# Four planned durations in the written-out order of a one-core transformer block: the exponential, the SiLU, GpSimd's power and GpSimd's products

## The chip, the cores and the metric

The kernel runs on one core of one Trainium2 chip. The core has a matrix engine (TensorE; PE in the profile, its weight loads PEld), a vector engine (VectorE, DVE), an activation engine (ScalarE, ACT), GpSimd (POOL) and SyncE (SP), which here issues DMAs alone. Each engine works through its own list of instructions in the order in which the program wrote them, and waits on semaphores where it needs another engine's result.

The metric is the device time of one execution in microseconds (us). Three runs before the change took 1913.58, 1913.61 and 1914.87 us; the median is 1913.61.

## The reference

One block with adaptive layer norms: attention over 2 batches of 2048 tokens of width 256, 16 heads with keys of 16 and values of 64, and a gated FFN of hidden width 704 whose inputs and weights are quantised to FP4 in blocks of 16.

```python
mod = (_silu(L0_c) @ L0_wmod).reshape(L0_c.shape[0], 6, 1, -1)
sa, ca, ga, sb, cb, gb = (mod[:, 0], ..., mod[:, 5])
...
h = _layernorm(x, axis=-1) * (1 + ca) + sa
x = x + ga * _L0_attn_ref(h, ...)
h = _layernorm(x, axis=-1) * (1 + cb) + sb
x = x + gb * _L0_ffn_ref(h, ...)

def _L0_attn_ref(x, query_proj, key_proj, value_proj, output_proj):
    q, k, v = ...
    sim = jnp.einsum('bnkh,bmhk->bnhm', q, k)
    attn = jax.nn.softmax(sim * scale, axis=1)      # over the queries
    o = jnp.einsum('bnhm,bmhv->bnhv', attn, v)
    return jnp.einsum('bnhv,dhv->bnd', o, output_proj)

def fp4_linear(x, w):
    return jnp.einsum('bsk,nk->bsn', fp4_quant_dequant(x), fp4_quant_dequant(w))

h = jax.nn.silu(fp4_linear(x, w_gate)) * fp4_linear(x, w_up)
return fp4_linear(h, w_down)
```

The softmax runs over the queries. So for a block of 128 keys of one head, all 2048 queries lie along one row, and the sum of exponentials belongs to the key.

## The kernel before

**The work.** The attention is 512 steps: 2 batches, 16 heads, 16 blocks of 128 keys. In one step (`step` and `scores`):

1. PE multiplies keys by queries, four score matmuls (`ps`) into two double PSUM banks of 1024 scores each, a half step per double bank. There are three such banks (room `s`).
2. DVE scales each half into the SBUF tile `e` (room `e`, five of them) and takes the row's minimum with it, in one pass: 1024 such passes.
3. POOL joins the two minima (`mn`).
4. ACT takes the exponential of the whole row of 2048 in place, with its sum `z` from the accumulator.
5. DVE takes the reciprocal `rz`, POOL scales the 64 values by it (`vn`).
6. PE multiplies `vn` by `e` into the output sums (`o`), eight matmuls in the trace.

All else is woven between these steps: the projections to q, k (`qk`) and v (`v`), copies of finished sums (`osb`), output projections (`op`), the weights' quantisation during the first batch, the second batch's first norms, and, during the second batch's attention, the first batch's FFN (`ffn_stats`, `ffn`: rows `gate`, `up`, `h2t`, `dn`, 16 tiles of 128 tokens). The second batch's FFN comes last, after the last step, with nothing beside it (`project_last`, `tail_norm`, `tail`, `tail_part`: rows `pg`, `pu`, `dn`).

**The order.** Every operation is a step of some generator, a `Chain`, with a due time counted in attention steps. `Order.run` is a planner that runs when the program is built. It keeps a clock for each engine, and for every chain whose next operation could go it works out the earliest start from the engine's clock, the end of the chain's last operation, a latency (0.2 us across engines) and a free room (a buffer). On each engine it looks at all that could start within a small time of the earliest (`patience`: PE 0.12, DVE 0.04, ACT 0.05 us) and takes the one due first. What it picks is emitted at once, so the order of the picks is the order of each engine's instructions. The chip then follows that order whatever its own durations are.

The planner's durations come from `Queue.estimate`, by engine, operation and size. Four more things hang on them:

- `scores` opens a visit to the scores with up to two half steps and lets it grow to three (`GROUP`), if a bank comes free within `PATIENCE` = 0.1 us of the time at which the visit would end.
- `Either` and `Best` give the planner a choice of engine: copies out of PSUM by ACT or DVE, products by POOL or DVE. `Best` takes the first unless it would end more than a margin later than the second. The margins are 0.5 us for copies and for the last FFN, 2 us for the first FFN and 3 us for the weights.
- SiLU and the exponential need different ACT tables. A change of table is planned at 1.3 us.
- An operation of POOL, and one of DVE with two inputs in SBUF (`shares`), reserves a shared `port` from its start to its planned end. Another such operation is not planned to start before that end.

**The operations whose planned duration the change touches.** The exponential is in `step` (an activation with a bias from SBUF and an accumulated sum). Two other activations accumulate: `Square` in `ffn_stats` and a copy in `projected`, both in the last FFN. SiLU stands in `ffn` (all 704 columns), `tail` (704) and `tail_part` (352). The power is in `inverse_root`: `G.tensor_tensor(r, v, half_root..., ALU.pow)` on 128 x 4, 128 x 3 or 128 x 1 numbers, from variance to the layer norm's root, followed at once by four small DVE operations (tiles `ln1`, `ln2`; `a` is the first norm, `f` the FFN's). POOL's products are all other `G.tensor_tensor`: in `quantize`, `quantize_exactly`, `ffn_apply`, `finish`, `load_wo` and `weight_tail`.

Each instruction that the planner emits bears the line of the call in `make`, L275; the tiles' names tell them apart.

## Time and profile before

| what | value |
|---|---|
| median of the runs | 1913.61 us |
| span of the profiled execution, first to last instruction | 1911.2 us |
| granted TensorE clock | 1.000 of full speed |
| exponential, 128 x 2048 | 512 times, mean 2003 ns, and 512 accumulator reads, mean 186 ns |
| SiLU, 704 columns, first FFN | 16 times, mean 757 ns |
| power, 128 x 4 | 15 times, means 1032 (first norms) and 1087 ns (FFN) |
| product on POOL, 128 x 704, plain and with a factor per block | means 1693 and 1390 ns |
| product on POOL, 128 x 256, plain and with a factor per block | means 733 and 623 ns |

An engine's busy time is the time in which an instruction of it was under way. Matmuls overlap in their pipeline, so a busy PE can still lose time between two kinds of matmuls. The rows of groups give the tiles written and read, the count, the busy time, the mean of one, and the idle time of the engine just before, with what ended it. Rows of the timeline give the start, the length, the engine, the line, the operation, the tiles and how many in a row were merged; a bracket at the end is the engine's idle time before it.

### The profile page before, as it was taken

The page shows a single profiled execution, that of the slowest core. Times are in us where ns is not written, and L with a number is a line of the kernel's source. Part 1 is how long each engine was busy: PE and PEld are TensorE (multiplying, and loading weights), DVE is VectorE, ACT ScalarE, POOL GpSimd, SP SyncE. Part 2 cuts the span into 40 slices and gives each one's busy share as a digit, 9 for nine tenths or more (in the row PEclk, how much of TensorE's full clock was granted, in tenths as well). Part 3 has the DMA queues.
Part 4 walks back from the last instruction along what each step waited for, and adds up shares of the span by engine and source line. Part 5 has one row for each costly group of instructions (what it writes and reads, how often), then busy time and mean ns, then how long its engine had stood idle before and what let it go on. Part 6 is the DMA issues. An engine that isn't in the chain of part 4 may idle for free.

```text
span 1911.2 us, 30108 instructions
## 1 busy us (share of the span) xinstructions
PE 1886.2 (99%) x10184; PEld 782.0 (41%) x10184; DVE 1691.7 (89%) x3975; ACT 1326.9 (69%) x1463; POOL 652.2 (34%) x1421
## 2 busy tenths in 40 slices
PE   9999999999999999999999999999999999999998
PEld 5333333343333333334334443434434333335666
DVE  5999999999999998888898788798788988997997
ACT  4687677776777677766777567766676867786433
POOL 1343333333334332113445345454353211231222
PEclk9999999999999999999999999999999999999999
DMA  6422021112120223211111201210111111101011
GB/s 215 104 63 56 30 55 49 45 27 51 34 60 21 51 56 94 78 39 45 31 37 48 61 31 47 51 42 10 39 37 37 42 34 34 34 7 39 9 17 20
DMA packets 42249, 89.83 MB, mean 47 GB/s; under 512 B 6384, under 2 KB 24432, under 8 KB 38128
## 3 DMA queue, kind: packets, MB, share of 16 engines
q1 hardware_dynamic: 38720, 83.97, 16.9%
q0 software_dynamic: 2016, 1.84, 0.8%
q10 hardware_dynamic: 1360, 2.10, 0.3%
q8 instruction: 81, 1.33, 0.3%
q14 instruction: 72, 0.59, 0.1%
HBM read 63.51 MB, written 22.81 MB: 45 GB/s over the span
## 4 chain that ended last, share of the span: by engine, by line
PE 88%; DVE 8%; ACT 2%; issue 1%; POOL 0%; ACTq 0%; POOLq 0%
PE o L275 44%; PE ps L275 15%; DVE e L275 6%; PE v L275 6%; PE op L275 5%; PE dn L275 5%; PE qk L275 3%; PE up L275 2%; PE pg L275 2%; PE gate L275 2%; PE pu L275 2%; PE h2t L275 1%; ACT e L275 1%; PE busy L275 1%; PE hq L275 0%
## 5 line engine op out<-in xcount | busy, mean ns | idle before, releaser
L275 DVE TENSOR_SCALAR_CACHE_REDUCE e<-ps 128x1024 f32<-128x1024 f32 x1024 | 1227.8, 1216 | 101.7 <-PE ps L275 82.4
L275 ACT ACTIVATE e<-e,mn 128x2048 f32<-128x2048 f32 x512 | 1025.2, 2003 | 401.4 <-POOL mn L275 397.7
L275 PE MATMUL o<-e,vn 128*64 128x512 f32 x4096 | 992.8, 603 | 6.7 <-POOL vn L275 2.9
L275 PEld LDWEIGHTS o<-e,vn 128*64 128x64 f32 x4096 | 255.9, 136 | 454.6 <-issue 371.4
L275 POOL TENSOR_SCALAR mn<-mn 128x1 f32<-128x1 f32 x512 | 154.2, 301 | 688.4 <-DVE rz L275 314.9
L275 PE MATMUL ps<-q,k 64*128 64x512 f32 x2048 | 369.0, 444 | 2.0 <-DVE e L275 1.6
L275 PEld LDWEIGHTS ps<-q,k 64*128 64x128 f32 x2048 | 160.2, 184 | 345.2 <-DVE e L275 132.3
L275 POOL TENSOR_SCALAR vn<-v,rz 128x64 f32<-128x64 f32 x512 | 166.5, 325 | 295.2 <-DVE rz L275 207.3
L275 PE MATMUL op<-wo,osb 128*64 128x256 f32 (+1 forms) x960 | 125.6, 382 | 1.2 <-DVE x L275 1.0
L275 PE MATMUL v<-wv,ht 128*64 128x256 f32 x1024 | 124.4, 382 | 0.3 <-DVE e L275 0.3
L275 PEld LDWEIGHTS op<-wo,osb 128*64 128x64 f32 (+1 forms) x960 | 74.1, 140 | 60.4 <-issue 22.2
L275 PEld LDWEIGHTS v<-wv,ht 128*64 128x64 f32 x1024 | 71.1, 137 | 65.5 <-issue 26.3
L275 DVE RECIPROCAL rz<-z 128x1 f32<-128x1 f32 x512 | 80.7, 158 | 18.8 <-ACT e L275 17.8
L275 ACT ACTIVATION_READ_ACCUMULATOR e<-e,mn 128x1 f32 x512 | 95.3, 186 | 0.0
L275 DVE DVE_READ_ACCUMULATOR e<-ps 128x1 f32 x1024 | 85.2, 83 | 0.0
L275 ACT COPY osb<-o 64x512 f32<-64x512 f32 x108 | 62.5, 580 | 14.9 <-PE o L275 13.4
L275 PE MATMUL qk<-ht,wqk_sb 128*64 128x512 f32 (+1 forms) x224 | 61.8, 599 | 1.1 <-ACT ht L275 0.9
L275 POOL TENSOR_TENSOR h<-h,m 128x704 f32<-128x704 f32 x32 | 54.2, 1693 | 12.3 <-DVE m L275 5.4
L275 DVE TENSOR_TENSOR x<-op,x 128x512 f32<-128x512 f32 (+1 forms) x59 | 39.8, 674 | 11.6 <-PE op L275 11.2
L275 PE MATMUL dn<-wdb,e 117*128 117x256 f32 (+1 forms) x192 | 45.1, 383 | 4.1 <-ACT e L275 4.0
L275 ACT ACT_TABLE_LOAD x34 | 43.6, 1283 | 4.3 <-issue 3.7
L275 PE MATMUL dn<-wd_t,h2t 117*64 117x256 f32 (+1 forms) x384 | 46.0, 381 | 0.0
(251 smaller groups left out, 1449.7 us busy)
## 6 DMA issues: line engine op xcount, KB each, us to landing
k<-scr SPq DMA_DIRECT2D x124, 256.0 KB, 4.5
scr<-st SPq DMA_DIRECT2D x32, 512.0 KB, 3.1
q<-scr SPq DMA_DIRECT2D x124, 128.0 KB, 5.5
x<-in_x_dram SPq DMA_DIRECT2D x8, 512.0 KB, 4.2
wv<-in_wv_dram SPq DMA_DIRECT2D x8, 256.0 KB, 3.6
wo<-in_wo_dram SPq DMA_DIRECT2D x8, 256.0 KB, 2.7
xt<-in_x_dram SPq DMA_DIRECT2D x4, 512.0 KB, 8.0
out_dram<-h2t SPq DMA_DIRECT2D x16, 128.0 KB, 1.9
```

The lines of the kernel that those rows point to most:

```text
L275: op = Op(self.name, *self.estimate(method, args, kw, lambda: f(*args, **kw)))
```

## The change

Four durations in `Queue.estimate` are replaced. With an accumulated sum an activation's planned duration grows by 0.11 us in place of 0.17. SiLU gets 0.148 us more. A power on POOL gets 1.0 us, whatever its size, where it had 0.08 us plus 0.0023 us a column, or 0.28 us for one column. The fixed part of all other tensor-tensor operations of POOL with more than one column goes from 0.08 to 0.11 us. Nothing else is changed: no operation, buffer, due time, margin or patience.

```diff
@@ -314,15 +314,18 @@
             func = kw.get("func", args[2] if method == "activation" else None)
             table = {AF.Exp: "exp", AF.Silu: "silu"}.get(func)
             t += 0.093 * sum(isinstance(kw.get(k), bass.AP) for k in ("bias", "scale"))
-            t += 0.17 * isinstance(kw.get("accum_out"), bass.AP)
+            t += 0.11 * isinstance(kw.get("accum_out"), bass.AP)
+            t += 0.148 * (func == AF.Silu)
             return t, emit, 0.0, table
         if self.name == "POOL":
             if method == "tensor_scalar":
                 return 0.16 + 0.083 * len(aps[2:]) + n * 0.001, emit
+            if ALU.pow in args:
+                return 1.0, emit
             if n == 1:
                 return 0.28, emit
             spread = any(len(a.ap) > 2 and a.ap[-1][0] == 0 for a in aps)
-            return 0.08 + n * (0.0019 if spread else 0.0023), emit
+            return 0.11 + n * (0.0019 if spread else 0.0023), emit
         if method == "reciprocal":
             return 0.07 + n * 0.0063, emit
         scalars = method == "tensor_scalar" and len(aps) > 2
```

## The prediction

> **What bounds the kernel now.** I read the page first: span, busy time, chain.

> ```profile
> span 1911.2 us, 30108 instructions
> PE 1886.2 (99%) x10184; PEld 782.0 (41%) x10184; DVE 1691.7 (89%) x3975; ACT 1326.9 (69%) x1463; POOL 652.2 (34%) x1421
> PE 88%; DVE 8%; ACT 2%; issue 1%; POOL 0%; ACTq 0%; POOLq 0%
> ```

> TensorE is never out of work for long. So the order in which its work is written out decides, not one slow engine. Next the busy time by stretch: the attention with all that is woven into it (50 to 1742 us), and two stretches of the last FFN.

> ```profile
> 50.00:1742.00 1692.00, 1682.98 (x9272) 640.45 (x9272) 1516.69 (x3502) 1236.55 (x1289) 610.63 (x1370) 1.00 0.17 45
> ...
> 1785.00:1830.00 45.00, 43.07 (x186) 31.10 (x185) 43.98 (x104) 19.83 (x39) 9.51 (x9) 1.00 0.13 15
> 1830.00:1870.00 40.00, 37.52 (x162) 27.27 (x161) 38.98 (x96) 14.14 (x23) 11.65 (x10) 1.00 0.12 14
> ```

> The columns after the length are PE, PEld, DVE, ACT, POOL. In the attention PE stands still for 9.0 us of 1692. In the last FFN DVE is the full engine: 82.96 of 85 us.

> What then fills the attention, if not waiting? The timeline shows turns between scores (ps) and weighted sums (o).

> ```profile
> 499.96 2.00 ACT L275 ACTIVATE e<-e,mn 128x2048 f32<-128x2048 f32 x1
> ...
> 501.46 0.96 PE L275 MATMUL ps<-q,k 64*128 64x512 f32 x6
> ...
> 501.87 0.19 ACT L275 ACTIVATION_READ_ACCUMULATOR e<-e,mn 128x1 f32 x1
> ...
> 502.35 2.80 PE L275 MATMUL o<-e,vn 128*64 128x512 f32 x12
> ...
> 505.08 1.07 PE L275 MATMUL ps<-q,k 64*128 64x512 f32 x6
> ...
> 508.80 0.73 PE L275 MATMUL ps<-q,k 64*128 64x512 f32 x4
> ...
> 509.46 1.94 PE L275 MATMUL o<-e,vn 128*64 128x512 f32 x8
> ```

> Six ps hold PE for 502.35 - 501.46 = 0.89 us, four for 509.46 - 508.80 = 0.66, so two cost 0.23 and a visit costs 0.66 - 0.46 = 0.20 on top. Twelve o last 2.80 and eight 1.94, so four cost 0.86; twelve (2.58) hold PE for 505.08 - 502.35 = 2.73, 0.15 on top. A turn to the scores and back thus costs 0.35 us. Counted over the whole timeline there are 462 visits to the scores (117 of six matmuls, 328 of four, 17 of two), 12 to 16 for each of the 32 heads: some 160 us.

> **The change part by part.** It gives the planner other costs and adds, removes and moves no instruction by itself: the same 30108 can come out in another order, and where two engines may do an operation the choice can flip. No DMA is added. A moved instruction moves SP's and POOL's queues with it, but no wait on a load stands among PE's waits after 50 us, so I cost that at nothing; if a head's load came late its cover is the stretch of some 16 steps by which it is issued ahead.

> Exponential: planned at 0.05 + 2048/1200 + 0.04 + 0.093 + 0.17 = 2.06 us, then 2.00. In the fence above the accumulator read ends 2.10 after the exponential began, but it overlaps: the next free moment of ACT comes after 501.87 - 499.96 = 1.91 plus about 0.09, so 2.00 is right for ACT's queue. For the reader behind it the last step shows it undisturbed: the exponential began at 1740.01, the reciprocal of its sum at 1742.14, 2.13 later; the plan allowed 2.06 + 0.20 and will allow 2.20. So 0.07 of cover is left of 0.13. What is late if the cover goes is vn on POOL, and then PE:

> ```profile
> PEld o L275 <- POOL vn L275: 27.4, 65, 1.7
> ...
> PE o L275 <- POOL vn L275: 2.9, 5, 1.3
> ```

> 65 times the weight load of an o began on the release by vn, so an o planned 0.06 earlier costs up to 65 x 0.06 = 3.9 us. The other end is a gain: ACT looks 512 x 0.06 = 31 us emptier to the planner, and copies may leave DVE for it; if one in ten of the 54 that DVE does from PSUM for v and osb (0.69 each) left, DVE would have 3.5 us less. I take +2.0, half of the first, since DVE's row is not PE's.

> Power: planned 0.09 us for the four-wide ones (0.28 for the one-wide), then 1.00. Measured 1.03 (17 in all; the three-wide 0.86, the one-wide 0.58). What planning it short does is seen here:

> ```profile
> 998.92 1.04 POOL L275 TENSOR_TENSOR ln1f<-ln0f,half_root 128x4 f32<-128x4 f32 x1 [0.81 <-DVE ln0f L275]
> ...
> 999.92 1.68 POOL L275 TENSOR_TENSOR h<-h,m 128x704 f32<-128x704 f32 x1
> 999.99 1.64 DVE L275 TENSOR_TENSOR ln2f<-ln1f 128x4 f32<-128x4 f32 x1 [1.15 <-POOL ln1f L275]
> ...
> 1002.83 0.50 PE L275 MATMUL ps<-q,k 64*128 64x512 f32 x2 [0.97 <-DVE e L275]
> ...
> 1003.97 0.49 PE L275 MATMUL ps<-q,k 64*128 64x512 f32 x2 [0.64 <-DVE e L275]
> ```

> DVE stood 1.15 us for the power with the next pass over scores queued behind it, then its small product took 1.64 beside a POOL product, and PE lost 0.97 + 0.64 = 1.61. With 1.00 planned, that pass goes ahead: -1.6. By tile, DVE waited for the power 3.0 us (5 times) in the FFN norms and 2.8 (3 times) in the first ones, so -5.8 is the lower end; the upper is the power in the first tile of the last FFN, planned 0.42 too long, which PE covers (its projections run until 1763.45, the tile is ready at 1759.83); uncovered, +0.4. I take -1.6, the only wait that reaches PE beyond doubt.

> The power also reserves the planner's shared port, now for 1.00 instead of 0.09 us, against DVE operations with two SBUF inputs. The row at 1762.77 shows a power of 1.02 us with such an operation of DVE (128x256) starting at 1763.25 and taking its usual 0.42: no block. [...]

> SiLU and products: SiLU 0.64 planned, then 0.79. Before a table load it holds ACT 0.77 (1002.57 to 1003.34), so 16 of them become truer; in the last FFN the next ACT operation came 0.64 after (1806.78 to 1807.42), so 17 become 0.15 too long. [...] Products become 0.03 longer: 1.73 planned against 1.69 measured (704 wide), 0.70 against 0.73 (256). In the last FFN POOL does 13 (seven e, six w) with a margin of 0.5 against DVE: a shift of 0.03 flips some 13 x 0.03/0.5 = 0.8 of them, and an e product on DVE takes 0.89 where DVE is full: +0.7. Ends: 0, and all seven, +6.2. In the attention DVE has 1692 - 1517 = 175 us of cover, so no term.

> New order: the planner takes the earliest start within 0.12 us and the lowest due time, so a shift of 0.06 in 512 steps redraws the attention's order. The trace has no row for a redraw; the nearest are its own heads. Taking each kind's mean spacing inside its stretches as streaming, a head loses 11 to 16 us outside it, with a spread (standard deviation) of 1.2 from head to head; over 30 heads that is 1.2 x root of 30 = 6.6. So -6.6 to +6.6. I take ten visits more, a third of one per head: 10 x 0.35 = +3.5. Two rows make me lean to loss. A third half of scores joins a visit only if DVE frees its bank within 0.1 us; banks come free every 1.22 us, so moving PE 0.06 earlier breaks 5% of the 117 visits of six, about six, which is three visits. And PE's waiting in the attention is only 9.0 us in all, so a redraw has little to win there and no such floor under what it may lose.

> Sum: 2.0 - 1.6 + 0.7 + 3.5 = +4.6. On the execution's own span: 1911.2 + 4.6 = 1915.8; the median of the runs shown, 1913.61, lies 2.4 above the span, so 1918.2.

> **The rivals.** Faster: the power's true length is the whole story. DVE's 5.8 us of standing before the root steps all reach PE, or the prologue's start (2.8 of them lie before 24 us, where PE has no scores yet): 1913.6 - 5.8 = 1907.8. It decides if visits to the scores stay at 462 or fall; each ten fewer give 3.5 more. Against it: of three waits in the first norms PE shows only 1.42 us for xn there.

> No change: the terms cancel and the redraw gives nothing: 2.0 - 1.6 + 0.7 = +1.1, 1914.7. That the changed costs hardly move any choice belongs here. For it: 9 us of waiting leave little to move. Against it: a sum of 30 heads seldom stays near zero.

> Slower by the last FFN alone: its chains plan SiLU 0.15 too long and all seven e products go to the full DVE: 7 x 0.89 = 6.2, 1919.8. Against it: ACT is half idle there, and the 0.5 margin still favours POOL.

> **How the numbers follow.** Forecast (more turns) 0.34; last FFN 0.11; no change 0.22; faster 0.33. Slower has 0.45. 0.2% is 3.8 us, about what a measurement here can tell from no change: 1909.8 to 1917.4 is the same. The slower cases alone span 1917.5 to 1930. The whole range takes the faster end, 1913.6 - 5.8 - 3.5 = 1904.3, so 1904, and at the top the upper ends 3.9 + 6.2 + 6.6 = 16.7, so 1930.

> **What would show it.** Visits of scores: 472 or so against 462; under 455 the forecast is wrong. DVE's wait of 1.15 before the root step near 1000 us gone. PE's loads on vn over 65. The seven e products on POOL: six or seven. PE's 9.0 us of waiting in the attention: a rise over 15 would mean waits, not turns, and a fall below 6 with fewer visits the faster rival.

## The result and the profile after

After the change the kernel takes 1921.88 us (median of four runs, 1921.67 to 1923.63), before 1913.78 (four runs beside it, 1913.58 to 1914.87). The ratio is 1.0042, 95% interval 1.0028 to 1.0056: slower by 8.1 us. The span of the profiled execution went from 1911.2 to 1919.9.

The page of the changed kernel, span and busy time:

```profile
span 1919.9 us, 30085 instructions
PE 1888.7 (98%) x10184; PEld 779.7 (41%) x10184; DVE 1694.3 (88%) x3983; ACT 1325.8 (69%) x1461; POOL 646.8 (34%) x1416
PE 11%; ACT 0%; issue 0%; DVE 0%; ACTq 0%
```

The same work in another order. In the last row the chain of waits was followed over 11% of the span only, so I don't read it, and compare stretches instead. The busy time by stretch of the changed kernel, columns as before (length, PE, PEld, DVE, ACT, POOL, granted clock, DMA):

```profile
50.00:1742.00 1692.00, 1678.71 (x9240) 636.22 (x9234) 1511.33 (x3486) 1229.94 (x1284) 611.36 (x1367) 1.00 0.18 44
1785.00:1830.00 45.00, 42.98 (x183) 30.75 (x182) 43.30 (x101) 17.23 (x27) 6.85 (x7) 1.00 0.11 13
1830.00:1870.00 40.00, 37.28 (x160) 26.52 (x159) 37.99 (x90) 16.59 (x33) 8.63 (x8) 1.00 0.15 17
```

PE now stands still for 13.3 us of these 1692 where it was 9.0. The two stretches don't hold the same work, as the changed order runs later. So, to see where, I cut each trace at PE's own events: the first score matmul, the first of head 13 and of head 16 (heads counted from 0 over both batches, so 16 is the second batch's first), and the last weighted sum.

| stage | before, us | after, us | PE idle before | after | visits before | after |
|---|---|---|---|---|---|---|
| up to the first scores | 38.4 | 40.9 | 4.2 | 3.9 | | |
| heads 0 to 12 | 643.3 | 638.5 | 4.7 | 4.0 | 187 | 191 |
| heads 13 to 15 | 159.0 | 168.4 | 2.0 | 8.4 | 45 | 46 |
| heads 16 to 31 | 904.7 | 904.6 | 2.6 | 2.1 | 230 | 234 |
| last FFN | 165.7 | 167.5 | 7.9 | 9.1 | | |

From the first scores to the last weighted sum PE stands still for 9.4 us before and 14.5 after. The start is 2.5 longer because the changed order puts 16 matmuls of v and two of the modulation ahead of the first scores. Heads 0 to 12, which no longer hold them, are 4.8 shorter. The loss is in heads 13 to 15: +9.4, of which 6.4 is PE standing still. About 1.0 more is four `o` and two transposes that stood in heads 0 to 12 before. Three stretches there, before and then after:

```profile
681.00:737.00 56.00, 53.99 (x278) 18.77 (x274) 49.65 (x122) 43.36 (x50) 17.65 (x42) 1.00 0.25 66
737.00:797.00 60.00, 60.00 (x302) 20.21 (x302) 50.21 (x101) 44.63 (x48) 12.22 (x40) 1.00 0.27 85
797.00:848.00 51.00, 51.00 (x312) 21.45 (x310) 40.95 (x83) 35.42 (x38) 9.04 (x31) 1.00 0.27 67
```

```profile
681.00:737.00 56.00, 51.74 (x270) 18.70 (x268) 50.59 (x122) 40.61 (x44) 15.41 (x39) 1.00 0.24 63
737.00:797.00 60.00, 57.59 (x284) 18.45 (x280) 43.68 (x88) 39.16 (x43) 10.88 (x34) 1.00 0.26 81
797.00:848.00 51.00, 49.27 (x292) 20.16 (x292) 43.41 (x87) 35.08 (x38) 9.12 (x31) 1.00 0.14 37
```

PE loses 2.25, 2.41 and 1.73 us, 6.4 together. In the middle stretch no engine is short of capacity: DVE too does less (43.68 against 50.21 busy). That is the mark of a pipeline that runs too shallow, where each engine waits for the next. The weight loads of the weighted sums say at which link (waits of the weight loads in 737 to 848, total, times, longest), before and then after:

```profile
PEld o L275 <- POOL vn L275: 1.1, 3, 0.4
```

```profile
PEld o L275 <- POOL vn L275: 8.8, 10, 1.9
```

And PE's rows of the timeline, after, in head 14:

```profile
768.72 1.08 PE L275 MATMUL o<-e,vn 128*64 128x512 f32 x4
769.88 0.49 PE L275 MATMUL ps<-q,k 64*128 64x512 f32 x2
...
770.98 1.94 PE L275 MATMUL o<-e,vn 128*64 128x512 f32 x8
773.57 1.08 PE L275 MATMUL o<-e,vn 128*64 128x512 f32 x4 [0.65 <-POOL vn L275]
774.58 0.73 PE L275 MATMUL ps<-q,k 64*128 64x512 f32 x4
775.24 1.94 PE L275 MATMUL qk<-ht,wqk_sb 128*64 128x512 f32 x8
```

PE has done all that was ready and waits for `vn` of the very next step. I put a number on this: the lead, by how many steps the scores already issued are ahead of the weighted sums when a step's first `o` begins, as a mean over a head.

| head | 12 | 13 | 14 | 15 |
|---|---|---|---|---|
| before | 3.78 | 3.47 | 4.41 | 4.91 |
| after | 3.41 | 3.50 | 3.00 | 4.56 |

Both orders lose lead in heads 12 and 13, where the second batch's norms and the last of the weights' quantisation are woven in (DVE is busy for 99% of head 12 in both). The order of before has it back in head 14. In the changed order it falls further in that stretch, to 3.0; there the second batch's `qk` take turns with the scores.

### The profile page after: what moved, and what is told of

Same layout as the page of the kernel before. It is cut to its first block, busy times and chain, and to the rows that moved or that the text cites. A ratio compares the mean times of both kernels' runs of the same rounds, so it can differ in the third digit from the quotient of the medians.

```text
span 1919.9 us, 30085 instructions
## 1 busy us (share of the span) xinstructions
PE 1888.7 (98%) x10184; PEld 779.7 (41%) x10184; DVE 1694.3 (88%) x3983; ACT 1325.8 (69%) x1461; POOL 646.8 (34%) x1416
## 5 line engine op out<-in xcount | busy, mean ns | idle before, releaser
L275 DVE TENSOR_SCALAR_CACHE_REDUCE e<-ps 128x1024 f32<-128x1024 f32 x1024 | 1227.0, 1216 | 102.9 <-PE ps L275 81.5
L275 ACT ACTIVATE e<-e,mn 128x2048 f32<-128x2048 f32 x512 | 1025.3, 2003 | 407.4 <-POOL mn L275 403.4
L275 PE MATMUL o<-e,vn 128*64 128x512 f32 x4096 | 994.4, 603 | 8.7 <-POOL vn L275 4.9
L275 PEld LDWEIGHTS o<-e,vn 128*64 128x64 f32 x4096 | 254.4, 136 | 459.5 <-issue 368.6
L275 POOL TENSOR_SCALAR mn<-mn 128x1 f32<-128x1 f32 x512 | 153.9, 301 | 683.7 <-DVE rz L275 287.4
L275 PE MATMUL ps<-q,k 64*128 64x512 f32 x2048 | 370.4, 444 | 0.7 <-DVE e L275 0.2
L275 PEld LDWEIGHTS ps<-q,k 64*128 64x128 f32 x2048 | 159.6, 184 | 345.5 <-DVE e L275 126.9
L275 POOL TENSOR_SCALAR vn<-v,rz 128x64 f32<-128x64 f32 x512 | 168.2, 328 | 333.2 <-DVE rz L275 224.5
L275 PE MATMUL v<-wv,ht 128*64 128x256 f32 x1024 | 124.0, 382 | 3.6 <-DVE rz L275 1.7
L275 PE MATMUL op<-wo,osb 128*64 128x256 f32 (+1 forms) x960 | 125.2, 382 | 1.5 <-DVE x L275 1.0
L275 DVE RECIPROCAL rz<-z 128x1 f32<-128x1 f32 x512 | 80.8, 158 | 27.1 <-ACT e L275 26.3
L275 PEld LDWEIGHTS op<-wo,osb 128*64 128x64 f32 (+1 forms) x960 | 74.2, 140 | 60.8 <-issue 23.5
L275 PEld LDWEIGHTS v<-wv,ht 128*64 128x64 f32 x1024 | 71.4, 137 | 66.9 <-issue 27.3
L275 ACT ACTIVATION_READ_ACCUMULATOR e<-e,mn 128x1 f32 x512 | 95.3, 186 | 0.0
L275 DVE DVE_READ_ACCUMULATOR e<-ps 128x1 f32 x1024 | 85.1, 83 | 0.0
L275 ACT COPY osb<-o 64x512 f32<-64x512 f32 x101 | 58.4, 579 | 19.6 <-PE o L275 18.0
L275 PE MATMUL qk<-ht,wqk_sb 128*64 128x512 f32 (+1 forms) x224 | 62.4, 602 | 2.6 <-DVE ht L275 1.1
L275 POOL TENSOR_TENSOR h<-h,m 128x704 f32<-128x704 f32 x32 | 54.3, 1696 | 13.6 <-DVE rz L275 6.4
L275 DVE TENSOR_TENSOR x<-op,x 128x512 f32<-128x512 f32 (+1 forms) x59 | 39.8, 675 | 16.2 <-PE op L275 15.8
L275 PE MATMUL dn<-wdb,e 117*128 117x256 f32 (+1 forms) x192 | 45.1, 383 | 4.0 <-ACT e L275 3.8
L275 PE MATMUL dn<-wd_t,h2t 117*64 117x256 f32 (+1 forms) x384 | 46.1, 380 | 0.0
```

The source lines that it names most:

```text
L275: op = Op(self.name, *self.estimate(method, args, kw, lambda: f(*args, **kw)))
```

## The experiments

**One part at a time.** Four kernels, each with one line of the change alone.

```diff
# only exponential
-            t += 0.17 * isinstance(kw.get("accum_out"), bass.AP)
+            t += 0.11 * isinstance(kw.get("accum_out"), bass.AP)
# only power
+            if ALU.pow in args:
+                return 1.0, emit
# only products
-            return 0.08 + n * (0.0019 if spread else 0.0023), emit
+            return 0.11 + n * (0.0019 if spread else 0.0023), emit
# only SiLU
+            t += 0.148 * (func == AF.Silu)
```

> Only the accumulated sum's 0.11 for 0.17. One lost stretch (A): the loss sits in heads 13 to 15 and is about the same size whichever edit tips the order there; if the exponential tips it, +5 to +9 us with heads 13 to 15 some 168 us long (159 before, 168 with all four), else within 3 us of before. Sizes add up (B): 512 exponentials carry nearly all of it, +6 to +8, spread over all heads. Turns (C, the prediction's): +3 to +4 with some 470 visits to the scores against 462.

> Only the power's 1.0. A: either heads 13 to 15 are tipped (+5 to +9) or what is left is the last FFN, where with all four POOL kept 3 of 7 products and it took 1.8 us longer: 0 to +3. B: 17 operations of 512 and more, under +1.5. The prediction's term for the power alone: -1.6, with DVE's wait near 1000 us gone.

> Only the products' 0.11 for 0.08. A: tipped or not, so +5 to +9 or within 3 us. B: 0.03 us on some 260 products, +1 at most. The prediction's term: +0.7, from products that go to DVE in the last FFN.

> Only SiLU's 0.148 more. Its first use is in the second batch's attention, after head 16, so heads 0 to 15 must have the same order as before and A allows no loss there: within 2 us. B: 33 operations, under +1. The prediction's term: part of +0.7.

| kernel | median, us | ratio, 95% interval | heads 13 to 15 | lead, head 14 | heads 16 to 31 | last FFN | visits |
|---|---|---|---|---|---|---|---|
| before | 1914.19 | | 159.0 | 4.41 | 904.7 | 165.7 | 462 |
| only exponential | 1921.37 | 1.0038 (1.0023 to 1.0053) | 167.5 | 3.00 | 905.6 | 165.6 | 463 |
| only power | 1914.62 | 1.0003 (0.9993 to 1.0012) | 160.0 | 4.41 | 902.5 | 168.8 | 466 |
| only products | 1923.57 | 1.0050 (1.0035 to 1.0065) | 168.1 | 3.00 | 904.1 | 165.6 | 465 |
| only SiLU | 1913.61 | 0.9999 (0.9989 to 1.0008) | 159.0 | 4.41 | 905.1 | 165.7 | 464 |
| all four | 1921.88 | 1.0042 (1.0028 to 1.0056) | 168.4 | 3.00 | 904.6 | 167.5 | 471 |

(The row of before gives the median beside these four; that of all four is from its own comparison. The stages are from the profiled executions.) The parts don't add: alone they come to 7.2 + 0.4 + 9.4 - 0.6 = +16.4, together +8.1. The exponential alone and the products alone each bring most of the loss of heads 13 to 15, at the same lead of 3.00, and with hardly more visits (463, 465) than before: PE stands still there for 6.7 and 7.1 us, against 8.4 with all four and 2.0 before. Some 1.8 us of their 167.5 and 168.1 are not the order's: in these two profiled executions TensorE's clock fell to half for 3.41 us (last section). So the loss isn't a price per exponential or per product; it is a state of the order that either edit tips it into. The power alone wins 2.2 us in heads 16 to 31 and pays 3.1 in the last FFN.

**Is it the size of the edit?** All four with the exponential 2 ns longer; and the exponential's edit half as large.

```diff
# all four, exponential 2 ns longer
-            t += 0.11 * isinstance(kw.get("accum_out"), bass.AP)
+            t += 0.112 * isinstance(kw.get("accum_out"), bass.AP)
# before, exponential's edit halved
-            t += 0.17 * isinstance(kw.get("accum_out"), bass.AP)
+            t += 0.14 * isinstance(kw.get("accum_out"), bass.AP)
```

> All four changes, but the accumulated sum planned at 0.112 instead of 0.110: 2 ns on the exponential. If the loss is one lost stretch whose order tips (A), this can tip it back: heads 13 to 15 some 159 us instead of 168, scores 4.4 steps or more ahead of the weighted sums in head 14 instead of 3.0, and a total of +0 to +4 us against before (what the last FFN loses to the power stays). If the durations' sizes matter (B), 2 ns on 512 operations is nothing: +8, and 168 us.

> Only the accumulated sum, moved half the way: 0.14 instead of 0.17 (0.11 alone gave +7.2 us). B: half of it, +3.6, spread over the heads. A: all or nothing: within 1.5 us of before with head 14 at about 4.4 steps ahead, or the full +6 to +9 with 3.0.

Two nanoseconds took the loss away: 1912.29 us against 1913.67, ratio 0.9992 (0.9982 to 1.0001), lead 4.59 in head 14, heads 13 to 15 in 159.2 us. The half edit gave 1914.77, ratio 1.0006 (0.9996 to 1.0015), lead 3.62, heads 13 to 15 in 161.3. That lies in between, so the loss isn't all or nothing, as I had expected of one lost stretch. The stretches of the kernel with 2 ns more, against those of the change above:

```profile
681.00:737.00 56.00, 53.99 (x290) 20.32 (x288) 51.82 (x126) 42.74 (x47) 14.82 (x39) 1.00 0.27 69
737.00:797.00 60.00, 59.85 (x296) 20.09 (x296) 49.58 (x99) 43.46 (x50) 12.01 (x38) 1.00 0.23 75
797.00:848.00 51.00, 51.00 (x308) 21.11 (x304) 40.95 (x83) 34.53 (x36) 8.73 (x30) 1.00 0.27 68
```

PE's standing still in the three falls from 8.4 to 2.2 us. This kernel has 470 visits to the scores, the changed one 471. So visits are not what costs the time.

**Is it the `qk` that keep the lead down?** The second batch's first `qk` are spread over 26 steps in place of 22, in the changed kernel and, as a control, in the kernel before.

```diff
-            spread_over([qk(b, 0, i, n) for n in range(NCH) for i in range(2)], s0 - 36, s0 - 14)
+            spread_over([qk(b, 0, i, n) for n in range(NCH) for i in range(2)], s0 - 36, s0 - 10)
```

> All four changes as they are, and the eight projections to the second batch's first q and k spread over 26 steps instead of 22 (due times from 36 to 10 steps before the second batch in place of 36 to 14). If the loss lives on these projections holding one of three score banks while scores are only 3.0 steps ahead (A), head 14 gets back to 4.4 or more steps, heads 13 to 15 to 158 to 162 us, and the total to +0 to +4 us. If the four durations make every step worse (B) or there are merely more visits (C), nothing changes: +7 to +9.

> The control: the kernel before with the same 26 steps. A: its head 14 had its 4.4 steps already, so nothing to win, within 1.5 us of before. Were the wider spread a gain by itself, it would show here as -3 us or more, and the run with all four would prove nothing.

The changed kernel fell to 1916.94, ratio to before 1.0018 (1.0009 to 1.0027); the control gave 1915.00, 1.0006 (0.9997 to 1.0016), so the spacing wins nothing by itself. The stretches of the changed kernel with wider spacing:

```profile
681.00:737.00 56.00, 51.75 (x270) 18.67 (x268) 50.50 (x122) 40.63 (x44) 15.26 (x39) 1.00 0.24 64
737.00:797.00 60.00, 59.88 (x302) 20.24 (x301) 50.70 (x101) 43.43 (x47) 12.06 (x38) 1.00 0.25 77
797.00:848.00 51.00, 51.00 (x308) 21.02 (x308) 42.59 (x85) 33.92 (x36) 8.66 (x30) 1.00 0.26 63
```

The first stretch is as in the changed kernel (51.75 against 51.74), the other two are as good as before; the lead in head 14 is 4.72. So of the 6.4 us of PE's standing still, 4.0 go with the wider spacing, and 2.2 are lost before it, in head 13, and stay: heads 13 to 15 take 163.2 us, a little over the 162 expected. This fits `qk` that hold a low lead down. It doesn't prove it, as the wider spacing is a redraw of that stretch too, and the 2 ns show that a redraw alone can bring the lead back.

**The power's two sides.** The power planned with 1.0 everywhere but in the last FFN, alone; then all four edits with that, and with the exponential 15 ns longer, to keep it off the tipping point.

```diff
# only power, not in the last FFN
+            if ALU.pow in args and ('ln1f1' not in out.tensor.name):
+                return 1.0, emit
# all four: that, and
-            t += 0.11 * isinstance(kw.get("accum_out"), bass.AP)
+            t += 0.125 * isinstance(kw.get("accum_out"), bass.AP)
```

> Only the power's 1.0, and not in the last FFN. The power alone gave +0.4 us, of which its last FFN took 3.1 us more than before's. If that and nothing else undid the prediction's gain of 1.6, this gives -1 to -3.5 us with a last FFN of about 165.7 us and DVE's wait near 1000 us gone. If the gain was never there, 0 +-1.

> A version meant to beat both: SiLU and products as in the change, the power 1.0 outside the last FFN, the accumulated sum at 0.125 (15 ns more than in the change). If what counts is head 14's lead and the last FFN's power, both mended here: 4.4 or more steps in head 14, heads 13 to 15 at 157 to 161 us, last FFN about 166, total -2 to -5 us against before. If the truer exponential is itself what pays or costs, it should lie by the version with 2 ns, at -1.4 +-1.

The first took 1911.78 us against 1914.18, ratio 0.9987 (0.9978 to 0.9996), with heads 16 to 31 in 902.9 us and the last FFN at 165.7 again. The second took 1909.71, ratio 0.9977 (0.9968 to 0.9987): faster than both kernels, by 4.5 us than the one before. Its start is 3.0 longer, it wins in heads 0 to 12 (637.7 against 643.3), keeps 159.1 in heads 13 to 15 at a lead of 4.59, and loses nothing in the last FFN (165.6).

What the power's true length does in the first FFN is seen in the kernel with the power alone, in the rows of the timeline that stand against those near 1000 us in the prediction:

```profile
999.27 1.03 POOL L275 TENSOR_TENSOR ln1f<-ln0f,half_root 128x4 f32<-128x4 f32 x1 [0.81 <-DVE ln0f L275]
...
1000.97 1.22 DVE L275 TENSOR_SCALAR_CACHE_REDUCE e<-ps 128x1024 f32<-128x1024 f32 x1
...
1003.93 1.23 DVE L275 TENSOR_SCALAR_CACHE_REDUCE e<-ps 128x1024 f32<-128x1024 f32 x1
...
1005.08 0.52 DVE L275 TENSOR_TENSOR ln2f<-ln1f 128x4 f32<-128x4 f32 x1
```

DVE no longer stands for 1.15 us: passes over scores go ahead of the root step, and PE's two waits for them are gone.

**Why the power costs in the last FFN.** Either its long reservation of the planner's shared port pushes DVE's operations back, or the later planned end of the norm's chain does. In the one kernel the power is planned with 1.0 everywhere, but in the last FFN the port is reserved for the old time; in the other its chain keeps the old time there and only the port is reserved for 1.0.

```diff
# both, where the operation is made
+            if ALU.pow in args and 'ln1f1' in args[0].tensor.name:
+                op.over = 1.0 - (0.28 if size(args[0]) == 1 else 0.08 + size(args[0]) * 0.0023)
# chain long, port short
-                self.port = t
+                self.port = t - getattr(ops[-1], "over", 0.0)
# chain short, port long
-                self.port = t
+                self.port = t + getattr(ops[-1], "over", 0.0)
```

> Only the power's duration is changed, to 1.0 us everywhere. In the last FFN the power's own queue and chain are planned with 1.0, but the shared port is reserved for the old short time alone. Until now: 1.0 everywhere left the last FFN at 168.8 us (before: 165.7), 1.0 everywhere but there left it at 165.7. Theory P (the long reservation of the port pushes DVE's two-input operations back in the last FFN): the last FFN is back near 165.7, the median some 2 to 3 us under the kernel before. Theory C (the later planned end of the norm's chain redraws the last FFN): 168 to 169, the median level with the kernel before. A third, that any change of that chain redraws it by some other amount, gives neither: a length between or outside the two.

> The complement: the power is planned at 1.0 everywhere but in the last FFN; there its queue and chain keep the old short duration, and only the shared port is reserved 1.0 us long. Theory P: the last FFN is 168 to 169 us long, the median level with the kernel before. Theory C: 165.7, the median 2 to 3 us under the kernel before. The third: neither, or both runs on the same side.

| the power in the last FFN | last FFN, us | PE idle in it | products `e`,`s_g` on POOL | median, us | ratio, 95% interval |
|---|---|---|---|---|---|
| chain short, port short (power alone, not in the last FFN) | 165.7 | 7.9 | 7 | 1911.78 | 0.9987 (0.9978 to 0.9996) |
| chain long, port long (power alone) | 168.8 | 10.6 | 8 | 1914.62 | 1.0003 (0.9993 to 1.0012) |
| chain long, port short | 169.9 | 11.0 | 6 | 1915.75 | 1.0009 (1.0000 to 1.0018) |
| chain short, port long | 168.1 | 9.6 | 3 | 1913.98 | 1.0000 (0.9991 to 1.0009) |

Neither theory: each half brings the loss by itself, 4.2 and 2.4 us. The last FFN too is redrawn by any change there, and of the redraws tried with the power's edit none kept before's 165.7. What in that order is worth the 2 to 4 us was not found.

## Why the prediction came out as it did

The direction was right and the size short: +4.6 forecast, +8.1 measured, inside the range. The mechanism given the most weight (0.34, against 0.33 for faster), a redrawn order in the attention, is what happened; its carrier was named wrongly. That the sum came out on the right side is luck in part: none of its terms was paid where it was put, and with 2 ns on one cost no loss is left.

**The order: turns.** Forecast were 472 visits for 462, and 471 came; the +3.5 they were to cost didn't. Heads 0 to 12 have four more and are 4.8 us shorter, heads 16 to 31 have four more and are 0.1 shorter, and of three kernels with 470 visits two are level with before or faster. PE's busy time from the first scores to the last weighted sum, with the 2.5 us of matmuls moved ahead counted back, is 1.8 us above before's with the change's nine visits more. But it is 0.8 and 1.2 below with eight more (exponential 2 ns and 15 ns longer), and 2.6 above with one more (exponential alone, 1.8 of lowered clock taken off). The step that failed is "I take ten visits more ... 10 x 0.35 = +3.5": no price per visit shows in the runs, so the count was no measure. The redraw's bounds of -6.6 to +6.6 held: from the first scores to the last weighted sum it went from 1707.1 to 1711.5 us, +4.4, as -4.8, +9.4 and -0.1, each rounded. But it was not a sum of thirty small draws; it was one stretch. The prediction's own test, that a rise of PE's waiting over 15 us would mean waits and not turns, read 13.3 (14.5 by PE's own events) and would have let turns stand: it set a limit for 1692 us on what sits in 160. The other sentence, that a redraw has no such floor under what it may lose, was the better one.

**The exponential's cover, +2.0.** The weight loads that began on `vn` rose from 65 to 71 as forecast (over 65), here in the waits of the changed kernel:

```profile
PEld o L275 <- POOL vn L275: 34.4, 71, 1.9
...
PE o L275 <- POOL vn L275: 4.9, 7, 1.1
DVE ln2f L275 <- POOL ln1f L275: 2.3, 4, 1.2
```

But of the rise of 7.0 us in the first row, 7.7 (1.1 to 8.8) lies in 737 to 848. Elsewhere there is no cover lost, and the same cost 2 ns longer gave 25.1 us, under before's 27.4. The term had no place; what it would have covered was the lead. The gain at its other end, copies leaving DVE, didn't come either: DVE does 57 of them where it did 54.

**The power, -1.6.** Alone it won 2.2 us in heads 16 to 31 (1.8 where the last FFN was left out), so row and mechanism were right. In the changed kernel nothing is left of it there (904.6 against 904.7): the last row above shows a DVE wait of up to 1.2 us still, now near 1014 us, where PE doesn't wait on it. The step that failed is the upper end for the last FFN, "covered by PE" and +0.4 if not: the power alone cost 3.1 there, and the change 1.8. I had costed the operation's own delay, while the edit redraws the order behind it. The faster rival, the power's true length as the whole story at -5.8, is out: the power gave -2.4 at best, with the last FFN left out.

**The products, +0.7.** Six or seven of the seven on POOL were expected to stay; three did, in the tile's row of the changed kernel:

```profile
L275 POOL TENSOR_TENSOR e<-e,s_g x3: 1378/1386/1389, 1850.0 to 1886.8; 128x704 f32<-128x704 f32 x3
```

Yet the flips are not the price: with the products alone six stay and the last FFN is at 165.6, and in the table above three on POOL go with 168.1 and eight with 168.8. The rival of the last FFN alone, seven products at 0.89 for +6.2, is out: that stage lost 1.8.

**SiLU, nothing.** So it was: 0.9999 (0.9989 to 1.0008). **The start** was missing from the sum: +2.5 from matmuls moved ahead, more than won back by head 13 (2.4 us earlier than before). Moved work is also most of what heads 0 to 12 win: 2.5 of their 4.8 are the matmuls ahead of the first scores, about 1.0 the four `o` and two transposes that come later, and 0.7 less standing still.

**Left open.** Which single pick tips the order at head 14; why all four edits and the power alone move matmuls ahead of the first scores and the exponential or the products alone don't; and 1.6 us or so of heads 13 to 15, where 6.4 of standing still, four more `o` and two transposes and one more visit don't make up 9.4.

## What to carry to other kernels

In a written-out order, truer planned durations are no gain by themselves: they are another draw, and 2 ns on one cost moved the time by 9.6 us. So after a change of costs try a few small perturbations of it before judging it. Look at the stage where the pipeline's lead is lowest, not at counts over the whole kernel; and when single parts of an edit sum to twice the whole, suspect one shared tipping point.

## What the runs showed of the hardware

**TensorE's clock fell to half for 3.41 us after standing still for 1.73 us in two executions, and stayed after the same in another.** At the boundary of heads 14 and 15, PE stood for 1.73 us in the changed kernel and in those with the exponential or the products alone. In the profiled execution of the exponential alone the clock fell after it (timeline, then 1 us stretches with the granted clock in the third column from the right):

```profile
804.65 3.06 PE L275 MATMUL v<-wv,ht 128*64 128x256 f32 x16 [1.73 <-DVE rz L275]
807.43 1.72 PE L275 MATMUL o<-e,vn 128*64 128x512 f32 x4
```

```profile
804.00:805.00 1.00, 0.35 (x4) 0.34 (x6) 1.00 (x4) 0.46 (x2) 0.33 (x2) 1.00 0.98 279
805.00:806.00 1.00, 1.00 (x10) 0.79 (x8) 1.00 (x3) 1.00 (x1) 0.25 (x1) 0.67 1.00 197
806.00:807.00 1.00, 1.00 (x7) 0.64 (x5) 0.86 (x2) 1.00 (x2) 0.00 (x0) 0.50 0.89 205
807.00:808.00 1.00, 1.00 (x6) 0.61 (x4) 0.16 (x1) 0.34 (x2) 0.60 (x2) 0.50 1.21 246
808.00:809.00 1.00, 1.00 (x4) 0.00 (x0) 0.00 (x0) 1.00 (x2) 0.00 (x0) 0.63 0.19 33
809.00:810.00 1.00, 1.00 (x10) 0.52 (x8) 0.30 (x1) 1.00 (x1) 0.00 (x0) 1.00 0.00 0
```

The same rows in the changed kernel's profiled execution, after the same idle time:

```profile
804.64 1.95 PE L275 MATMUL v<-wv,ht 128*64 128x256 f32 x16 [1.73 <-DVE rz L275]
806.39 1.06 PE L275 MATMUL o<-e,vn 128*64 128x512 f32 x4
```

The clock stays at 1.00 there. At the lower clock the two rows together took (3.06 - 1.95) + (1.72 - 1.06) = 1.8 us longer in the one execution than in the other. With the products alone the clock fell too (0.78 and 0.88 in the stretches 805 to 810 and 810 to 815). It happened at another place as well, in the profiled execution of the control with the wider `qk`, after the two waits near 1003 us that the prediction shows for the kernel before:

```profile
1003.02 0.50 PE L275 MATMUL ps<-q,k 64*128 64x512 f32 x2 [0.99 <-DVE e L275]
1004.16 0.50 PE L275 MATMUL ps<-q,k 64*128 64x512 f32 x2 [0.65 <-DVE e L275]
1004.60 1.98 PE L275 MATMUL o<-e,vn 128*64 128x512 f32 x4
1006.36 3.37 PE L275 MATMUL up<-wu_t,hqt 128*64 128x352 f32 x16
```

In the kernel before, where the clock stayed at 1.00, the same groups read:

```profile
1004.39 1.08 PE L275 MATMUL o<-e,vn 128*64 128x512 f32 x4
1005.30 2.54 PE L275 MATMUL up<-wu_t,hqt 128*64 128x352 f32 x16
```

**Two DVE products of 128 x 4 ended with a GpSimd product, at 1.64 and 0.52 us; beside two powers DVE took its usual time.** A DVE product of 128 x 4 took 1.64 us at 999.99 in the kernel before, beside a POOL product from 999.92 to 1001.60; 0.52 at 1005.08 with the power alone, beside one that ended at 1005.57; and 0.16 at 1013.79 in the changed kernel, with POOL idle. In both of the first it ended with POOL's product, to 0.03 us. It wasn't so beside every product: in the kernel before, the DVE operation that writes `q_g` from `s_g` and `am_g` (128 x 44) took 0.74 at 1314.59 and ended with a POOL product of 128 x 256 begun at 1314.54, to 0.06 us, and 0.20 at 1210.17 beside one from 1210.15 to 1210.96. The row at 1762.77 in the prediction shows a power: in its 1.02 us a DVE operation took its usual 0.42. So does the changed kernel at 1848.00: a DVE product of 128 x 704 took its usual 0.88 beside a power from 1847.29 to 1848.64.
